# Two layers of graph attention on one core: PSUM banks swapped by batch parity, the order of pieces changed around projection, v and gather

## The chip, the cores and the metric

One core of a Trainium2 chip. The metric is the device time of the whole program in microseconds (us), as the median of several runs. The engines are named as in the profile: PE (TensorE), PEld (its weight loads), DVE (VectorE), ACT (ScalarE), POOL (GpSimd), SPq (the queue that issues DMAs).

## The reference, cut to what matters

Two residual layers with layer norm over 32 batches of 512 nodes and 512 features. The first is a graph layer (`l0` below), the second 8-head attention with a mask.

```python
# layer 0
mi = einsum('bkd,od->bko', x, Wi); mj = einsum('bkd,od->bko', x, Wj)
deg = a.sum(axis=1)
x = layernorm(x + deg[None, :, None] * (mi + b) + einsum('ij,bjo->bio', a, mj))
# layer 1: q, k, v = h @ W*.T + b*, 8 heads of 64
scores = where(adj == 0, -inf, q k^T / 8); attn = softmax(scores)
x = layernorm(x + (attn v) @ Wo.T + bo)
```

## The kernel before

Each 512x512x512 product (l0, q, k, v, output projection "pj") is done with seven half-size products, the **pieces** 1, 2, 6, 7, 4, 5, 3, in that order. Pieces {1, 2}, {6, 7, 4} and {5, 3} each add up in one PSUM bank; after each piece the bank is read by ACT or DVE before the next piece may write there. Two banks, "a" and "b", are all that pieces and gathers have. Weights of a piece come through a ring of 12 tiles in SBUF; its DMAs are issued by SPq in order, each waiting until the piece that used the tile is done.

Attention of batch b runs in 8 steps (two per head pair). Each step has scores, `exp` (ACT), mask (DVE) and attention times v ("ov" tiles); between them, PE does the pieces of batches n and n - 2 of the other layer parts. The list of pieces is cut into these 8 steps by the pieces' summed cost, so a piece that is moved can fall into another step.

Names used below: k6 is piece 6 of the product k; p1 is the copy of piece 1 that later pieces add; POOL's "differences" are the operands of the pieces; HT and OT are h and the attention output, turned (transposed); `base` is DVE's x + deg b, the start of the l0 output. "By starts" means that a pause is the time from one row's start to the next, less the undisturbed time. A "restart" is the 0.10 us that the piece behind a pause takes longer. "Half clock" is a stretch in which the trace records a granted TensorE clock of 0.5; nearly all are 3.41 us long or a multiple of it.

The parts that the argument touches, with cuts marked `# ...`:

```python
def load_x(b):
    XT[b] = work([P, NC, D], "xh", 3)
    nc.sync.dma_start(XT[b], rows(x[b]))

def l0_gather(b, dc, adjT=None):          # x^T, and A x in two fp32r halves
    pt = turn_tile()
    for jc in range(NC):
        nc.tensor.transpose(pt[...], xt[:, jc, dc * P:(dc + 1) * P], ident)     # L292
    nc.vector.tensor_mul(XD[b][:, dc, :], pt, deg_r)
    pm = mm_tile("b")
    # ... 4 matmuls with the rounded half xhi, 4 with the rest xlo (L299)
    nc.scalar.copy(AX_T[b][:, dc, :], pm)

def phase_a(n):     # gather of batch n among the last five k pieces of batch n - 1
    # ...
    for i in range(max(len(g), len(k))):
        res += k[i:i + 1] + g[i:i + 1]                                          # k in bank a, g in b

def phase_c(n):
    # ...
    res = [norm[0], norm[1], z(apply, n, 1)] if n else []
    res += [pc("v", n, 1, "a"), pc("q", n, 1, "b")]
    # ...
    for i in ORDER[2:]:                                                         # 6, 7, 4, 5, 3
        for f in pc("q", n, i, "b"), pc("v", n, i, "a"):
            res += [f] + [g for g in side[:1] if g]
            side = side[1:]
        if i == 5 and n + 1 < B:
            res += [z(load_x, n + 1)] if n > 0 else []                          # the load of the next batch
    if n + 1 < B:
        res += [z(ahead, n + 1)]                                                # casts of its first two blocks
    return res
```

Of the kernel before, what the change touches and what calls it, by code (L numbers as in the profile page):

```python
# [25 lines left out]
def gnn_attention_kernel(  # L26
# [57 lines left out]
    def mm_tile(bank):  # L84
        return psum.tile([P, 512], FT, name="mm" + bank, bufs=1)
# [194 lines left out]
        for ic in range(2 * half, 2 * half + 2):  # L280
            ln_apply(MV.pop((b, ic)), XT[b][:, ic, :])

    def l0_gather(b, dc, adjT=None):


        xt = XT[b]
        if dc == 0:
            XD[b] = big()
            AX_T[b] = big()
        pt = turn_tile()  # L290
        for jc in range(NC):
            nc.tensor.transpose(pt[:, jc * P:(jc + 1) * P], xt[:, jc, dc * P:(dc + 1) * P], ident)  # L292
        nc.vector.tensor_mul(XD[b][:, dc, :], pt, deg_r)  # L293
        pm = mm_tile("b")
        if adjT is None:
            parts = SPLIT.pop((b, dc))
            for w in range(2):
                for jc in range(NC):
                    nc.tensor.matmul(pm, parts[w][:, jc, :], adjR[:, jc, :],  # L299
                                     start=(w == 0 and jc == 0), stop=(w == 1 and jc == NC - 1))  # L300
        else:
            for jc in range(NC):
                nc.tensor.matmul(pm, xt[:, jc, dc * P:(dc + 1) * P], adjT[:, jc, :],
                                 start=(jc == 0), stop=(jc == NC - 1))
        nc.scalar.copy(AX_T[b][:, dc, :], pm)
        if adjT is None and dc + 2 < DC:
            split(b, dc + 2)
# [126 lines left out]
    def presum(hp, half):  # L434

        if half == 0:
            ES[hp] = work([P, 2, N], "es", 1)
            nc.gpsimd.tensor_add(ES[hp], E[0], E[1])  # L438
        else:
            for kc in (2, 3):  # L440
                nc.vector.tensor_add(ES[hp], ES[hp], E[kc])  # L441

    def values(b, hp, half):
        if half == 0:
# [27 lines left out]
        nc.vector.tensor_mul(OT[b, hp // 2][:, hp % 2, :], PV[hp], RL[hp][1])  # L472

    def rest(b, hp):
        return [(invert, b, hp, c) for c in range(4)] + [(tell, b, hp), (scale, b, hp)]

    def store(b):
        nc.sync.dma_start(rows(out[b]), XT.pop(b))
# [6 lines left out]
    def z(f, *a):  # L485
        return (0.0, f, *a)
# [4 lines left out]
    ORDER = (1, 2, 6, 7, 4, 5, 3)  # L491
    ALONE = ((1, "a"), (6, "b"), (2, "a"), (7, "b"), (5, "a"), (4, "b"), (3, "a"))

    def phase_a(n):

        g = [(TR + GA, l0_gather, n, dc) for dc in range(DC)] if n < B else []
        k = [pc("k", n - 1, i, "a") for i in ORDER[2:]] if n > 0 else []
        res = []
        for i in range(max(len(g), len(k))):
            res += k[i:i + 1] + g[i:i + 1]  # L500
            if n == 1 and i in (1, 3):
                res += [z(combine, "wo", nc.vector, i // 2)]
            if i == 1 and g:
                res += [z(combos, TX, n, lambda j, m: quarter(XD[n], j, m), (1,)),
                        z(combos, TA, n, lambda j, m: quarter(AX_T[n], j, m), (1,))]
        if g:
            res += [z(combos, TX, n, lambda j, m: quarter(XD[n], j, m), (2,)),
                    z(combos, TA, n, lambda j, m: quarter(AX_T[n], j, m), (2,)),
                    z(base, n, 0),
                    z(combos, TX, n, lambda j, m: quarter(XD[n], j, m), (3, 4)),  # L510
                    z(combos, TA, n, lambda j, m: quarter(AX_T[n], j, m), (3, 4)),
                    z(base, n, 1)]
        if n == 1:
            res += [z(fold)]
        return res

    def first():


        g = [(TR + GA, l0_gather, 0, dc) for dc in range(DC)]  # L520
        half = lambda name, i: z(combine, name, nc.gpsimd if name in ("wi", "wj") else nc.vector, i)
        y = [(8 * PC / 4, plain, ic) for ic in range(NC)]
        n = [(TR, l0_norm, 0, ic) for ic in range(NC)]
        return [g[0], z(graph_forms, 3), g[1], g[2], half("wv", 0), g[3], z(base, 0, 0), z(base, 0, 1), half("wv", 1),
                y[0], half("wq", 0), half("wi", 0), y[1], half("wq", 1), half("wi", 1), y[2], half("wk", 0), half("wj", 0),
                n[0], y[3], half("wk", 1), half("wj", 1), n[1]]

    def plain(ic):

        pm = mm_tile("ab"[ic % 2])  # L530
        c = slice(ic * P, (ic + 1) * P)
        for j, (t, w) in enumerate(((XD[0], W["wi"]), (AX_T[0], W["wj"]))):
            for dc in range(DC):
                nc.tensor.matmul(pm, t[:, dc, c], w[dc // 2][:, dc % 2, :], start=(j + dc == 0), stop=(j == 1 and dc == DC - 1))
        y = XT[0][:, ic, :]
        nc.vector.tensor_add(y, y, pm)
        mv = work([P, 5], "mv", 12)
        ln_stats(mv, y)
        ln_apply(mv, y)

    def project(m, i):

        res = [pc("pj", m, i, "b")]
        if i == 1:
            res = [z(combos, TO, m, ot_quarter(m), (1,))] + res
        if i == 2:
            res = [FLUSH] + res + [z(combos, TO, m, ot_quarter(m), (2, 3, 4))]
        return res

    def phase_b(n):  # L550

        m = n - 2
        if m < 0:
            res = []
            side = [z(add_bo, 0, i) for i in range(2)]
            for i, bank in (ALONE[0:1] + ALONE[2:3] + ALONE[1:2] + ALONE[3:]):
                res.append(pc("l0", n, i, bank))
                if i == 4:
                    res += [z(stats, n, 0)]
                res += side[:1]  # L560
                side = side[1:]
            return res + [z(apply, n, 0), z(stats, n, 1)]
        res = []
        for i in ORDER:
            res.append(pc("l0", n, i, "a"))
            if i == 4:
                res.append(z(stats, n, 0))
            if i == 5:
                res.append(z(stats, m, 0))
            if i == 3:  # L570
                res.append(z(stats, n, 1))
            res += project(m, i)
            if i == 4:
                res.append(z(apply, n, 0))
            if i in (7, 4):
                res.append(z(add_bo, n - 1, int(i == 4)))
        return res

    def phase_c(n):

        m = n - 2
        norm = [(TR, l0_norm, n, ic) for ic in range(NC)]
        h = lambda j, i: quarter(HT[n], j, i)
        res = [norm[0], norm[1], z(apply, n, 1)] if n else []
        res += [pc("v", n, 1, "a"), pc("q", n, 1, "b")]
        if m >= 0:
            res += [z(stats, m, 1)]
        res += [pc("v", n, 2, "a"), norm[2], norm[3], z(combos, TH, n, h, (1, 2)), pc("k", n, 1, "a"),
                z(combos, TH, n, h, (3, 4)), pc("q", n, 2, "b"), pc("k", n, 2, "a")]
        side = []  # L590
        if n == 0:

            side = [z(graph_forms, 2), None, z(graph_forms, 0), None, z(graph_forms, 1)]
        if m >= 0:
            res += [z(apply, m, 0), z(apply, m, 1), z(store, m)]
        for i in ORDER[2:]:
            for f in pc("q", n, i, "b"), pc("v", n, i, "a"):
                res += [f] + [g for g in side[:1] if g]
                side = side[1:]
            if i == 5 and n + 1 < B:  # L600
                res += [z(load_x, n + 1)] if n > 0 else []
        if n + 1 < B:
            res += [z(ahead, n + 1)]
        return res

    def fold():

        pd = mm_tile("b")
        bv_w = work([P, DC, P], "big", 6)
        for dc in range(DC):  # L610
            nc.vector.tensor_scalar(bv_w[:, dc, :], ones, bv_c[:, dc:dc + 1], None, op0=OP.mult)
            nc.tensor.matmul(pd, bv_w[:, dc, :], W["wo"][dc // 2][:, dc % 2, :], start=(dc == 0), stop=(dc == DC - 1))
        nc.vector.tensor_add(bo_r, bo_r, pd)

    def by_steps(todo):
        total, done, at, res = sum(f[0] for f in todo), 0.0, 0, []
# [68 lines left out]
    for n in range(1, B + 1):  # L685
        b = n - 1
        extra = []
        for step in range(STEPS):
# [9 lines left out]
            elif b > 0:  # L698
                values(b - 1, HP - 1, 1)
                sums(b - 1, HP - 1)  # L700
                extra = rest(b - 1, HP - 1)
            late = [(presum, hp, half)]
            for f in PERIODS[n][step]:
                if f is FLUSH:
                    some = len(extra)
                else:
                    run(f)

                    some = 0 if f[0] == 0.0 else len(extra) if step == 0 else max(1, round(f[0] / PC))
                if some:  # L710
                    for g in late + extra[:some]:
                        g[0](*g[1:])
                    late, extra = [], extra[some:]
            for g in late + extra:
                g[0](*g[1:])
            extra = []
# [15 lines left out]
    with tc.If(flag > 0), tc.tile_pool(name="general", bufs=1) as pools.work:  # L732
# [26 lines left out]
        with tc.For_i(0, B, 1) as b:  # L759
# [1 line left out]
            xt = XT[g] = work([P, NC, D], "xh", 1)  # L761
            nc.sync.dma_start(xt, x[bass.ds(b, 1)].rearrange("o (c p) d -> p (o c) d", p=P))
            for dc in range(DC):
                l0_gather(g, dc, adj_t)
            base(g, 0)
            base(g, 1)
            for ic in range(NC):
# [98 lines left out]
```

## Time and profile before

| | before |
|---|---|
| median of runs | 3995.48 us (3993.76 to 3996.59, 4 runs) |
| PE, DVE, POOL, ACT busy | 97, 65, 46, 27% |
| one steady batch, load to load | 122.41 us (mean of 29) |
| PE waiting for x in it | 0 |
| half-clock windows in the steady part | none |

PE is the bound. How it is read, and which pauses PE has, stands in the prediction with its lines. PE's recurring waits, from the list of waits before (total us of idle, times, longest), in the order k6, v2, q5, v1 and projection 2:

```profile
PE mma L375 <- DVE v L403: 24.2, 31, 0.8
PE mma L375 <- ACT p L382: 20.6, 30, 0.7
PE mmb L375 <- DVE q L418: 15.3, 30, 0.5
PE mma L375 <- ACT big L321: 10.9, 30, 4.0
...
PE mmb L375 <- DVE oT L472: 4.7, 30, 0.2
```

One caution for reading on: a row of the timeline gives a busy length that overlaps the next row (a piece is shown as 1.89 us but takes 1.73 from start to start), so pauses below are worked out from starts, and the bracket at the end of a row (idle before it) comes out some 0.17 us smaller.

### The profile page before, as it was taken

What the parts mean: (1) busy time and instruction counts of PE and PEld (TensorE: products, weight loads), DVE (VectorE), ACT (ScalarE), POOL (GpSimd) and SP (SyncE); (2) the same over time, 40 slices, a digit from 0 to 9 for tenths busy, and PEclk for the clock granted to TensorE, in tenths of its full rate; (3) what the DMA queues carried; (4) which work ended last, traced back from release to release, by engine and by line L of the source; (5) the groups of instructions that cost most, each with busy time, mean ns of one, the idle gap of its engine ahead of it and who ended that gap; (6) DMA issues with size and microseconds to landing.
All of it is one profiled execution on the core that took longest, in us unless ns stands there. A gap on an engine that the chain in (4) does not pass through costs nothing.

```text
span 3992.5 us, 46921 instructions
## 1 busy us (share of the span) xinstructions
PE 3869.0 (97%) x17370; PEld 2641.8 (66%) x17370; DVE 2611.4 (65%) x3525; ACT 1058.9 (27%) x1476; POOL 1846.2 (46%) x1861
## 2 busy tenths in 40 slices
PE   8999999999999999999999999999999999999997
PEld 6666666666666666666666666666666666666663
DVE  4566666666666666666666666666666666666666
ACT  2222222222322222222223222222222222222222
POOL 3354434544444544345444455443454434554433
PEclk9999999999999999999999999999999999999998
DMA  7323333333333333332333433333323333333330
GB/s 248 94 91 116 106 111 119 93 108 111 106 116 106 98 111 111 108 119 87 114 109 103 124 100 103 107 111 111 117 89 116 104 108 122 100 101 111 107 107 22
DMA packets 281865, 433.87 MB, mean 109 GB/s; under 512 B 23072, under 2 KB 119840, under 8 KB 281632
## 3 DMA queue, kind: packets, MB, share of 16 engines
q1 hardware_dynamic: 281376, 430.27, 35.0%
q8 instruction: 142, 2.33, 0.2%
q14 instruction: 91, 0.75, 0.1%
q0 software_dynamic: 256, 0.53, 0.0%
HBM read 389.29 MB, written 41.42 MB: 108 GB/s over the span
## 4 chain that ended last, share of the span: by engine, by line
PE 75%; DVE 18%; POOL 3%; issue 2%; ACT 2%; DMA 0%; SPq 0%; POOLq 0%
PE mma L375 31%; PE mmb L375 14%; PE sc L427 10%; PE ov L449 9%; PE mmb L299 6%; DVE xh L312 5%; DVE e L432 4%; DVE rl L462 3%; PE ov L456 2%; DVE es L441 2%; PE sc L292 1%; POOL mv L268 1%; DVE st L265 1%; POOL mv L267 1%; PE sc L320 1%
## 5 line engine op out<-in xcount | busy, mean ns | idle before, releaser
L375 PE MATMUL mma<-ring,big 128*128 128x256 f32 x5224 | 1216.3, 382 | 31.7 <-ACT p L382 20.6
L375 PEld LDWEIGHTS mma<-ring,big 128*128 128x128 f32 x5224 | 979.6, 190 | 255.9 <-DVE e L432 49.5
L431 ACT ACTIVATE sc<-sc 128x1024 f32<-128x1024 f32 x512 | 492.7, 1006 | 1546.0 <-PE sc L427 1467.6
L432 DVE TENSOR_TENSOR e<-sc,edge 128x1024 f32<-128x1024 f32 x512 | 602.7, 1218 | 368.7 <-ACT sc L431 368.7
L438 POOL TENSOR_TENSOR es<-e 128x1024 f32<-128x1024 f32 x128 | 301.6, 2356 | 896.4 <-PE ov L456 894.5
L344 POOL TENSOR_TENSOR big<-big 128x512 f32<-128x512 f32 x376 | 511.6, 1385 | 217.8 <-DVE big L293 195.8
L427 PE MATMUL sc<-q,k 64*128 64x512 f32 x2048 | 508.9, 615 | 0.2 <-ACT big L321 0.2
L449 PE MATMUL ov<-e,v 128*64 128x512 f32 x2048 | 497.6, 607 | 6.5 <-DVE told L467 6.5
L462 DVE RECIPROCAL rl<-ov 128x128 f32<-128x128 f32 x512 | 455.0, 924 | 5.4 <-PE ov L456 1.6
L375 PE MATMUL mma<-big,ring 128*128 128x256 f32 x1792 | 430.2, 383 | 27.9 <-DVE v L403 24.2
L375 PE MATMUL mmb<-big,ring 128*128 128x256 f32 x1792 | 427.8, 382 | 15.3 <-DVE q L418 15.3
L375 PEld LDWEIGHTS mma<-big,ring 128*128 128x128 f32 x1792 | 331.9, 190 | 111.5 <-DVE v L403 36.7
L375 PEld LDWEIGHTS mmb<-big,ring 128*128 128x128 f32 x1792 | 339.0, 190 | 73.3 <-DVE q L418 27.3
L267 POOL TENSOR_SCALAR mv<-mv 128x1 f32<-128x1 f32 x256 | 80.8, 316 | 618.0 <-DVE mv L266 604.4
L449 PEld LDWEIGHTS ov<-e,v 128*64 128x64 f32 x2048 | 124.6, 136 | 347.6 <-issue 294.8
L441 DVE TENSOR_TENSOR es<-es,e 128x1024 f32<-128x1024 f32 x256 | 326.8, 1277 | 4.4
L427 PEld LDWEIGHTS sc<-q,k 64*128 64x128 f32 x2048 | 176.1, 186 | 209.3 <-issue 195.8
L390 POOL TENSOR_TENSOR xh<-xh,p 128x512 f32<-128x512 f32 x186 | 230.6, 1268 | 117.4 <-ACT p L382 117.4
L393 DVE TENSOR_TENSOR xh<-xh,mma 128x512 f32<-128x512 f32 x186 | 125.7, 676 | 225.5 <-PE mma L375 220.0
L184 POOL TENSOR_TENSOR xlo<-xh,xhi 128x512 fp32r<-128x512 f32 x128 | 162.7, 1281 | 238.7 <-ACT xhi L183 238.7
L272 ACT ACTIVATE xh<-xh,mv 128x512 f32<-128x512 f32 x256 | 198.4, 811 | 240.2 <-POOL mv L269 224.6
L375 PE MATMUL mmb<-ring,big 128*128 128x256 f32 x1032 | 251.6, 387 | 4.9 <-POOL big L344 4.9
(125 smaller groups left out, 3696.3 us busy)
## 6 DMA issues: line engine op xcount, KB each, us to landing
ring<-wq SPq DMA_DIRECT2D x160, 256.0 KB, 2.6
ring<-wv SPq DMA_DIRECT2D x160, 256.0 KB, 2.6
ring<-wk SPq DMA_DIRECT2D x160, 256.0 KB, 4.1
ring<-wi SPq DMA_DIRECT2D x155, 256.0 KB, 2.6
ring<-wj SPq DMA_DIRECT2D x155, 256.0 KB, 2.8
ring<-wo SPq DMA_DIRECT2D x155, 256.0 KB, 2.6
xh<-in_x_dram SPq DMA_DIRECT2D x32, 1024.0 KB, 5.5
out_dram<-xh SPq DMA_DIRECT2D x31, 1024.0 KB, 5.1
```

The costliest lines, as they stand in the source:

```text
L299: nc.tensor.matmul(pm, parts[w][:, jc, :], adjR[:, jc, :], start=(w == 0 and jc == 0), stop=(w == 1 and jc == NC - 1))
L312: nc.vector.scalar_tensor_tensor(y, b0_r, deg_c[:, ic:ic + 1], y, op0=OP.mult, op1=OP.add)
L344: nc.gpsimd.tensor_tensor(dst, p, q, op=OP.subtract)
L375: nc.tensor.matmul(pm[:, c * Q:(c + 1) * Q], lhs, rhs, start=first, stop=(kc == 1 and n == len(terms) - 1), skip_group_check=True)
L390: nc.gpsimd.tensor_tensor(d, d, p1, op=OP.add)
L427: nc.tensor.matmul(ps[:, s, :], KT[b, hp // 2][r, hp % 2, kc * P:(kc + 1) * P], QT[b, hp // 2][r, hp % 2, :], start=True, stop=True)
L431: nc.scalar.activation(ps, ps, AF.Exp, scale=QSCALE)
L432: nc.vector.tensor_tensor(e, ps, edge[:, kc:kc + 1, :].to_broadcast([P, 2, N]), op=OP.mult)
L438: nc.gpsimd.tensor_add(ES[hp], E[0], E[1])
L441: nc.vector.tensor_add(ES[hp], ES[hp], E[kc])
L449: nc.tensor.matmul(PV[hp][s * HD:(s + 1) * HD, :], V[b][:, kc, c0:c0 + HD], E[kc][:, s, :], start=(kc == 0), stop=(kc == NC - 1))
L462: nc.vector.reciprocal(rl[:, c], pl[:, c])
```

## The change

Its intent is to take away PE's small recurring pauses: banks swap roles with each batch's parity, so that between the last v piece and the first k piece (k6), which share a bank, the gather of the next batch runs in the other one; the first two blocks of h are turned during the output projection, not right ahead of v; the first l0 piece moves ahead of the last k; v's bias is folded into the output bias early; DVE's two sums of a head pair are emitted one at a time; and the scaling of the attention output goes ahead of its check ("tell"). Cut to the core:

```diff
+    def banks(n):
+        return ("a", "b") if n % 2 == 0 else ("b", "a")
 # phase_a: g in bank A, k in bank K
-            res += k[i:i + 1] + g[i:i + 1]
+            res += g[i:i + 1] + k[i:i + 1]
 # ...
+        return res + [ ... z(base, n, 1), pc("l0", n, 1, A), k[4]]
 # phase_b
+            if i == 3:
+                res += [z(stats, n, 1), (TR, l0_norm, n, 1)]
+            if i == 5:
+                res.append((TR, l0_norm, n, 0))
 # phase_c
-        res = [norm[0], norm[1], z(apply, n, 1)] if n else []
-        res += [pc("v", n, 1, "a"), pc("q", n, 1, "b")]
+        res = [pc("v", n, 1, A)] + ([z(apply, n, 1)] if n else []) + [pc("q", n, 1, K)]
 # rest
-        ... + [(tell, b, hp), (scale, b, hp)]
+        ... + [(scale, b, hp), (tell, b, hp)]
 # steps
-            late = [(presum, hp, half)]
+            late = [(presum, hp, 0)] if half == 0 else [(presum, hp, 2), (presum, hp, 3)]
 # first(): fold of v's bias ahead of the first v, in place of the end of phase_a(1)
```

More of the change, by code (lines that the diff above doesn't have):

```diff
@@ L281, in apply, with l0_gather @@
             ln_apply(MV.pop((b, ic)), XT[b][:, ic, :])
-    def l0_gather(b, dc, adjT=None):
+    def l0_gather(b, dc, bank, adjT=None):
         xt = XT[b]
@@ L293, in l0_gather @@
         nc.vector.tensor_mul(XD[b][:, dc, :], pt, deg_r)
-        pm = mm_tile("b")
+        pm = mm_tile(bank)
         if adjT is None:
@@ L439, in presum @@
         else:
-            for kc in (2, 3):
-                nc.vector.tensor_add(ES[hp], ES[hp], E[kc])
+            nc.vector.tensor_add(ES[hp], ES[hp], E[half])
     def values(b, hp, half):
@@ L474, in rest @@
     def rest(b, hp):
-        return [(invert, b, hp, c) for c in range(4)] + [(tell, b, hp), (scale, b, hp)]
+        return [(invert, b, hp, c) for c in range(4)] + [(scale, b, hp), (tell, b, hp)]
     def store(b):
@@ L492, in gnn_attention_kernel @@
     ALONE = ((1, "a"), (6, "b"), (2, "a"), (7, "b"), (5, "a"), (4, "b"), (3, "a"))
+    def banks(n):
+        return ("a", "b") if n % 2 == 0 else ("b", "a")
     def phase_a(n):
-        g = [(TR + GA, l0_gather, n, dc) for dc in range(DC)] if n < B else []
-        k = [pc("k", n - 1, i, "a") for i in ORDER[2:]] if n > 0 else []
+        A, K = banks(n)
+        if n == B:
+            return [pc("k", n - 1, i, bank) for i, bank in ((6, K), (7, K), (5, A), (4, K), (3, A))]
+        xq, aq = lambda j, m: quarter(XD[n], j, m), lambda j, m: quarter(AX_T[n], j, m)
+        g = [(TR + GA, l0_gather, n, dc, A) for dc in range(DC)]
+        k = [pc("k", n - 1, i, K) for i in ORDER[2:]]
         res = []
-        for i in range(max(len(g), len(k))):
-            res += k[i:i + 1] + g[i:i + 1]
+        for i in range(DC):
+            res += g[i:i + 1] + k[i:i + 1]
             if n == 1 and i in (1, 3):
                 res += [z(combine, "wo", nc.vector, i // 2)]
-            if i == 1 and g:
-                res += [z(combos, TX, n, lambda j, m: quarter(XD[n], j, m), (1,)),
-                        z(combos, TA, n, lambda j, m: quarter(AX_T[n], j, m), (1,))]
-        if g:
-            res += [z(combos, TX, n, lambda j, m: quarter(XD[n], j, m), (2,)),
-                    z(combos, TA, n, lambda j, m: quarter(AX_T[n], j, m), (2,)),
-                    z(base, n, 0),
-                    z(combos, TX, n, lambda j, m: quarter(XD[n], j, m), (3, 4)),
-                    z(combos, TA, n, lambda j, m: quarter(AX_T[n], j, m), (3, 4)),
-                    z(base, n, 1)]
-        if n == 1:
-            res += [z(fold)]
-        return res
+            if i == 1:
+                res += [z(combos, TX, n, xq, (1,)), z(combos, TA, n, aq, (1,))]
+        return res + [z(combos, TX, n, xq, (2,)), z(combos, TA, n, aq, (2,)), z(base, n, 0),
+                      z(combos, TX, n, xq, (3, 4)), z(combos, TA, n, aq, (3, 4)), z(base, n, 1),
+                      pc("l0", n, 1, A), k[4]]
     def first():
-        g = [(TR + GA, l0_gather, 0, dc) for dc in range(DC)]
+        g = [(TR + GA, l0_gather, 0, dc, "b") for dc in range(DC)]
         half = lambda name, i: z(combine, name, nc.gpsimd if name in ("wi", "wj") else nc.vector, i)
@@ L524, in first @@
         return [g[0], z(graph_forms, 3), g[1], g[2], half("wv", 0), g[3], z(base, 0, 0), z(base, 0, 1), half("wv", 1),
-                y[0], half("wq", 0), half("wi", 0), y[1], half("wq", 1), half("wi", 1), y[2], half("wk", 0), half("wj", 0),
-                n[0], y[3], half("wk", 1), half("wj", 1), n[1]]
+                y[0], z(scaled, 0), half("wq", 0), half("wi", 0), y[1], z(scaled, 1), half("wq", 1), half("wi", 1), z(fold, 0), y[2], half("wk", 0), half("wj", 0),
+                z(scaled, 2), n[0], y[3], half("wk", 1), half("wj", 1), n[1], (2 * PC, fold, 1), z(scaled, 3)]
     def plain(ic):
@@ L536, in plain, with scaled @@
         nc.vector.tensor_add(y, y, pm)
-        mv = work([P, 5], "mv", 12)
-        ln_stats(mv, y)
-        ln_apply(mv, y)
+        MV[0, ic] = work([P, 5], "mv", 12)
+        ln_stats(MV[0, ic], y)
+    def scaled(ic):
+        ln_apply(MV.pop((0, ic)), XT[0][:, ic, :])
     def project(m, i):
-        res = [pc("pj", m, i, "b")]
+        res = [pc("pj", m, i, banks(m)[1])]
         if i == 1:
@@ L555, in phase_b @@
             side = [z(add_bo, 0, i) for i in range(2)]
-            for i, bank in (ALONE[0:1] + ALONE[2:3] + ALONE[1:2] + ALONE[3:]):
+            A, K = banks(n)
+            for i, bank in ((2, A), (6, K), (5, A), (7, K), (3, A), (4, K)):
                 res.append(pc("l0", n, i, bank))
@@ L561, in phase_b @@
                 side = side[1:]
-            return res + [z(apply, n, 0), z(stats, n, 1)]
-        res = []
-        for i in ORDER:
-            res.append(pc("l0", n, i, "a"))
+            return res + [z(apply, n, 0), z(stats, n, 1), (TR, l0_norm, n, 0), (TR, l0_norm, n, 1)]
+        res = project(m, 1)
+        for i in ORDER[1:]:
+            res.append(pc("l0", n, i, banks(n)[0]))
             if i == 4:
@@ L570, in phase_b @@
             if i == 3:
-                res.append(z(stats, n, 1))
+                res += [z(stats, n, 1), (TR, l0_norm, n, 1)]
             res += project(m, i)
@@ L583, in phase_c @@
         h = lambda j, i: quarter(HT[n], j, i)
-        res = [norm[0], norm[1], z(apply, n, 1)] if n else []
-        res += [pc("v", n, 1, "a"), pc("q", n, 1, "b")]
+        A, K = banks(n)
+        res = [pc("v", n, 1, A)] + ([z(apply, n, 1)] if n else []) + [pc("q", n, 1, K)]
         if m >= 0:
             res += [z(stats, m, 1)]
-        res += [pc("v", n, 2, "a"), norm[2], norm[3], z(combos, TH, n, h, (1, 2)), pc("k", n, 1, "a"),
-                z(combos, TH, n, h, (3, 4)), pc("q", n, 2, "b"), pc("k", n, 2, "a")]
+        res += [pc("v", n, 2, A), norm[2], norm[3], z(combos, TH, n, h, (1, 2)), pc("k", n, 1, A),
+                z(combos, TH, n, h, (3, 4)), pc("q", n, 2, K), pc("k", n, 2, A)]
         side = []
@@ L596, in phase_c @@
         for i in ORDER[2:]:
-            for f in pc("q", n, i, "b"), pc("v", n, i, "a"):
+            for f in pc("q", n, i, K), pc("v", n, i, A):
                 res += [f] + [g for g in side[:1] if g]
@@ L604, in phase_c, with fold @@
         return res
-    def fold():
-        pd = mm_tile("b")
-        bv_w = work([P, DC, P], "big", 6)
-        for dc in range(DC):
-            nc.vector.tensor_scalar(bv_w[:, dc, :], ones, bv_c[:, dc:dc + 1], None, op0=OP.mult)
-            nc.tensor.matmul(pd, bv_w[:, dc, :], W["wo"][dc // 2][:, dc % 2, :], start=(dc == 0), stop=(dc == DC - 1))
-        nc.vector.tensor_add(bo_r, bo_r, pd)
+    def fold(part):
+        if part == 0:
+            bv_w = OPEN["fold"] = work([P, DC, P], "rl", 1)
+            for dc in range(DC):
+                nc.vector.tensor_scalar(bv_w[:, dc, :], ones, bv_c[:, dc:dc + 1], None, op0=OP.mult)
+        else:
+            pd = ov_tile()
+            for dc in range(DC):
+                nc.tensor.matmul(pd, OPEN["fold"][:, dc, :], W["wo"][dc // 2][:, dc % 2, :], start=(dc == 0), stop=(dc == DC - 1))
+            nc.vector.tensor_add(bo_r, bo_r, pd)
     def by_steps(todo):
@@ L710, in gnn_attention_kernel @@
                 if some:
-                    for g in late + extra[:some]:
+                    for g in late[:1] + extra[:some]:
                         g[0](*g[1:])
-                    late, extra = [], extra[some:]
+                    late, extra = late[1:], extra[some:]
             for g in late + extra:
@@ L763, in gnn_attention_kernel @@
             for dc in range(DC):
-                l0_gather(g, dc, adj_t)
+                l0_gather(g, dc, "b", adj_t)
             base(g, 0)
```

## The prediction

> **What bounds the kernel now.** I read the page first (shares, then the chain), then the timeline of TensorE (PE) in one steady batch, then the DVE, ACT and issue-queue (SPq) timelines at the places where PE paused.
>
> ```profile
> PE 3869.0 (97%) x17370; PEld 2641.8 (66%) x17370; DVE 2611.4 (65%) x3525; ACT 1058.9 (27%) x1476; POOL 1846.2 (46%) x1861
> ...
> PE 75%; DVE 18%; POOL 3%; issue 2%; ACT 2%; DMA 0%; SPq 0%; POOLq 0%
> ```
>
> PE is the bound. No other engine is above 65%, and no DMA is on the chain, so the time is PE's issue rate plus its pauses. From one x load to the next the trace repeats every 122.35 us. The change removes no matmuls in a batch; only pauses can change. The PE timeline round the x load (start, length; each x8 row is one "piece" of four fp32 matmuls):
>
> ```profile
> 1293.22 1.89 PE L375 MATMUL mma<-ring,big 128*128 128x256 f32 x8
> 1295.62 1.99 PE L375 MATMUL mmb<-big,ring 128*128 128x256 f32 x8 [0.51 <-DVE q L418]
> 1297.45 1.89 PE L375 MATMUL mma<-ring,big 128*128 128x256 f32 x8
> 1299.17 1.89 PE L375 MATMUL mmb<-big,ring 128*128 128x256 f32 x8
> 1300.99 1.99 PE L427 MATMUL sc<-q,k 64*128 64x512 f32 x8
> ...
> 1305.64 1.99 PE L375 MATMUL mma<-ring,big 128*128 128x256 f32 x8
> 1308.41 1.99 PE L375 MATMUL mma<-big,ring 128*128 128x256 f32 x8 [0.78 <-DVE v L403]
> 1310.24 0.60 PE L292 MATMUL sc<-ident,xh 128*128 128x128 f32 x4
> ```
>
> These rows are v4, q5, v5, q3, scores, v3, k6 and the transposes of the next batch's x. An undisturbed piece takes 1.73 us start to start (1297.45 to 1299.17). After v3 it is 2.77: k6 takes v3's bank and waits for its last read. Every pause also makes the next piece 1.83 instead of 1.73. Measured start to start over the free pace, a steady batch has five pauses: k6 0.94, v2 0.85 (waits for p1's copy), q5 0.67, v1 0.40 (waits for HT's copy), output projection 2 0.32 (waits for OT). That is 3.18, with five restarts of 0.10 some 3.7 us per batch. The changes of array shape around scores and values remain.
>
> **The skill.** "TensorE: Matmul & The Clock Gate", in "Step-by-step: what each phase is for", says that matmuls stay in program order and only weight loads are pulled ahead: one that waits for data holds all behind it. The trace agrees: k6's 0.94 delays everything after it. The same page, "What's actually happening", says that PE's clock is halved after an idle window of about 3.4 us. Here the 3.95 us pause at 54 us is followed by a piece of 2.94 us start to start (59.54 to 62.48) instead of 1.73, and the recorded half-clock stretches are 3.413 us or multiples. Cutting the span into such windows, those with PE busy 34% or less were followed by half clock, those with 49% or more were not. "DMA: Bandwidth & Descriptors", "Rules for kernel authors": issue a load early, wait late. The kernel before does so by little, see below.
>
> **The change part by part (per steady batch, 30 of them).**
>
> *Removed.* Banks by parity: after v3 comes the gather of the next batch (2.28 us: 0.35 transposes, 1.02 and 0.91 matmuls) in the other bank, so k6 finds v3's bank read: -0.94 -0.10. First two blocks of h turned during the projection: v1 no longer follows the HT copy directly, -0.40 -0.10, and the apply pair (2 x 0.81 on ACT) is put behind p1's copy, so v2 doesn't wait: -0.85 -0.10. q5 now stands one step later behind scores and values (3.8 us) and v4, and DVE's two sums of 1.24 are apart: -0.67 -0.10. Sum -3.26.
>
> *OT.* Scaling ahead of the tell saves 0.61 on DVE (the tell starts at 1220.78, the product behind it at 1221.39). But the first l0 piece (3.45 us) moved from between the sums and projection 2 to the end of the batch before. From the scores' start: base (6.27 us on DVE) now starts before that l0 piece and ends at about 3.4; k3's reads 0.9, masks 2.3, four reciprocals 3.4, product 0.65: 10.6. PE wants it at 10.15 (1.92 + 1.77 + 0.96 + 1.83 + 3.45 + 0.2). Pause 0.5 to 0.6 instead of 0.32: **+0.25**.
>
> *q1.* Step 3 now opens with a transpose, and one sum goes behind it and ahead of the read of projection 3. In DVE's row at this place:
>
> ```profile
> 1258.84 2.36 DVE L432 TENSOR_TENSOR e<-sc,edge 128x1024 f32<-128x1024 f32 x2 [0.17 <-ACT sc L431]
> 1261.11 0.68 DVE L265 BATCH_NORM_STATS2 st<-xh 128x6 f32<-128x512 f32 x1
> ...
> 1262.72 0.65 DVE L393 TENSOR_TENSOR xh<-xh,mmb 128x512 f32<-128x512 f32 x1
> 1263.30 2.48 DVE L441 TENSOR_TENSOR es<-es,e 128x1024 f32<-128x1024 f32 x2
> ```
>
> the read (L393) stands before both sums; after, it stands behind one. Masks end 4.75 us after the scores' start, statistics 6.3, sum 7.55, read 8.1. q1 takes the bank that the projection left, and PE is there at 7.8 (1.92 + 1.87 + 0.44 + 1.83 + 1.73). **+0.4 +0.1.**
>
> *The x load.* This is what I believe decides. The load is issued after v5 in both kernels, in order with the weight prefetches, the last of which waits for v5's matmuls:
>
> ```profile
> 1299.37 0.37 SPq L253 DMA_DIRECT2D ring<-in_wjT_dram  x1
> 1299.85 0.41 SPq L107 DMA_DIRECT2D xh<-in_x_dram  x1
> ```
>
> ACT's cast of it, and the page's row of this load (KB each, median us to landing):
>
> ```profile
> 1305.28 1.14 ACT L183 CAST xhi<-xh 128x512 fp32r<-128x512 f32 x2 [1.18 <-DMA xh<-in_x_dram]
> ...
> xh<-in_x_dram SPq DMA_DIRECT2D x32, 1024.0 KB, 5.5
> ```
>
> Issue is 0.68 after q3's start; it lands 5.2 to 7.3 us later in the steady part, mean about 5.65. Before, PE reaches the transposes 10.4 us after the issue, because scores, values, sums (4.65), v3 and k6 lie between: nobody waits. After, the built order on PE is v4, q5, v5, q3, v3, gather: PE is there 3.45 us after q3's start, 2.77 after the issue. Pause 5.65 + 0.1 - 2.77 = 2.95. Then the transposes (0.35) run while ACT casts the first half (0.62): +0.3; and POOL's subtraction (1.27) ends 0.3 after the first four gather matmuls: +0.3. Restart 0.1. **+3.65.** Such a gap leaves many a 3.4 us window under about 40% busy: a gap of 2.95 with 0.3 behind it does so in about 80% of the positions of the window, and a half-clock window costs up to 1.7, partly inside the gap, say 1.3. **+1.0.**
>
> Rest (norm 1 against the first mask, projection 6 against POOL's difference): +0.1.
>
> Sum per batch: -3.26 + 0.25 + 0.5 + 3.65 + 1.0 + 0.1 = +2.2; times 30 = **+67 us**.
>
> *Start and end.* Before, v's bias is folded alone behind base:
>
> ```profile
> 115.10 6.12 PE L612 MATMUL mmb<-xh,big 128*128 128x512 f32 x8 [7.75 <-DVE big L611]
> ```
>
> 7.9 us of pause, and 6.12 instead of 3.43 at half clock. Folded ahead of the first v, it also fills the 3.95 us pause that the first v has at 54 us (4.1 start to start, 1.7 of half clock behind it). At most -16; at the end two of the last k's waits (1.15 each) go with alternating banks: -2. I take **-18**.
>
> 3996.6 + 67 - 18 = 4045.6; I put 4044.
>
> **The rivals.** (1) *The pauses go and nothing comes.* Then 3996.6 - 18 - 30 x 3.3 = 3880, -2.9%. For it: the intended effects are sound. Against it: it needs the load to land within 2.8 us of the issue; the fastest of the steady part took 5.2. (2) *The load waits, but the clock holds and q1 and OT pass.* Then -3.26 + 3.65 + 0.1 = +0.5 per batch: 3994. Steady pauses before were never over 1 us, so the steady part tells nothing of the clock; only start and end do. (3) *DVE becomes the bound.* Its order changes in steps 0, 3 and 7, and each queue slips by up to one op (1.2 us) more than I worked out: +2 per batch more, 4105. For it: the two DVE chains above are longer than PE's time. Against it: DVE is busy 65% and stands idle in between. (4) *The weight ring*: same number of transfers of 2.6 us, same depth of 12; nothing changes there.
>
> **Range and chances.** The load's wait is nearly certain in kind; its size is 3.1 to 4.2. The clock adds 0 to 1.7, DVE's two places 0.2 to 1.6. Per batch +0.5 to +3.2 about, 80% range 4005 to 4080. Over 2% slower begins at 4076.5: 0.16. Over 2% faster would need rival 1: 0.04.
>
> **What would show it.** The first transposes (L292) of a batch idle about 3 us before them, ended by the x load, 30 times, about 90 us in all; the wait for k6 on v's last read, and those of v2 and v1, gone from the list of waits; ACT's cast then within 0.1 us of the transposes; half-clock windows (tenths under 9 or a mean granted clock near 0.98) in the steady part; a wait of q1 on the projection's read of 0.4; bias fold without 7.75 us. The prediction is wrong if the load lands earlier than the transposes, if PE has no gap there, or if the period of a batch comes out under 122.35.

## The result, and the profile after

4048.32 us (4046.68 to 4050.38, 4 runs) against 3995.48: ratio 1.0133, 95% interval 1.0115 to 1.015. Ratios here are the mean time of one kernel's runs over that of the other's of the same rounds, so not quite the ratio of the medians. The change is slower, by 53 us: clear of the noise, though under 2%.

The page of the profile after, busy times and the chain that ended last, by engine and by line:

```profile
PE 3902.1 (96%) x17370; PEld 2663.9 (66%) x17370; DVE 2595.3 (64%) x3525; ACT 1058.3 (26%) x1476; POOL 1862.8 (46%) x1861
...
PE 72%; DVE 11%; POOL 9%; DMA 4%; issue 2%; ACT 1%; SPq 0%; POOLq 0%
PE mma L375 20%; PE mmb L375 20%; PE sc L427 10%; PE ov L448 9%; POOL xh L390 5%; DMA xh<-in_x_dram 4%; PE mmb L299 3%; PE mma L299 3%; DVE rl L461 3%; PE ov L455 2%; DVE st L265 2%; DVE xh L393 2%; POOL big L344 2%; DVE e L432 2%; POOL es L438 2%
```

As many matmuls as before, but a DMA has come onto the chain with 4% of the span: the load of x. Its place in PE's timeline of one batch (start, length):

```profile
1180.76 1.89 PE L375 MATMUL mmb<-ring,big 128*128 128x256 f32 x8
1182.48 1.89 PE L375 MATMUL mma<-big,ring 128*128 128x256 f32 x8
1184.21 1.89 PE L375 MATMUL mmb<-ring,big 128*128 128x256 f32 x8
1188.77 1.11 PE L292 MATMUL sc<-ident,xh 128*128 128x128 f32 x4 [2.67 <-DMA xh<-in_x_dram]
1189.53 2.06 PE L299 MATMUL mma<-adjR,xhi 128*128 128x512 f32 x4
1191.39 1.24 PE L299 MATMUL mma<-adjR,xlo 128*128 128x512 f32 x4
```

The issue queue and ACT at the same place:

```profile
1182.68 0.37 SPq L253 DMA_DIRECT2D ring<-in_wjT_dram  x1
1183.14 0.42 SPq L107 DMA_DIRECT2D xh<-in_x_dram  x1
```

```profile
1188.75 1.14 ACT L183 CAST xhi<-xh 128x512 fp32r<-128x512 f32 x2 [12.23 <-DMA xh<-in_x_dram]
```

These are v5, q3, v3 and then the gather. The load is issued as before, 0.66 us after q3's start. PE is done with v3 at 1185.94 (1184.21 + 1.73), the load lands at 1188.72, and the transposes start at 1188.77: 2.83 us of pause. The first matmuls of the gather then take 1.86 us where they took 1.01 before (1310.60 to 1311.61 there): a half-clock window stands behind the gap.

The recurring waits for p1, for q5's bank, for k6's bank and for HT that stood in the list before are gone. PE's recurring waits in the list of the kernel after are these. None of them recurs in the list before (POOL's L344 stands there once, at the end, with 4.9); OT's wait goes on, but is too short for this list:

```profile
PE sc L292 <- DMA xh<-in_x_dram: 89.3, 30, 5.5
...
PE mmb L375 <- POOL big L344: 7.9, 15, 5.0
...
PE mma L375 <- POOL big L344: 2.9, 14, 0.2
PE mmb L375 <- DVE xh L393: 2.4, 15, 0.2
PE mma L375 <- DVE xh L393: 2.2, 14, 0.2
```

By the trace's starts, the x wait is 3.13 us per batch (2.45 to 5.65). 21 of the 29 steady batches have a half-clock stretch at the gap (3.41 us, or 6.83 in three). Where a batch has none, its length less its own x wait is the same every time, which separates the wait from the clock (load to load, us):

| length | x wait | difference |
|---|---|---|
| 123.37 | 2.61 | 120.76 |
| 123.85 | 3.08 | 120.77 |
| 123.33 | 2.61 | 120.72 |
| 123.47 | 2.73 | 120.74 |
| 123.77 | 3.01 | 120.76 |
| 123.32 | 2.56 | 120.76 |

So a batch costs 120.74 (the mean of all eight such batches) + the x wait. The mean of all is 124.62 = 120.74 + 3.13 + 0.75, and 0.75 is the half clock: 1.04 us for each of the 21 batches that have it.

### The profile page after: what moved, and what is told of

Same layout as the page of the kernel before. It is cut to its first block, busy times and chain, and to the rows that moved or that the text cites. A ratio compares the mean times of both kernels' runs of the same rounds, so it can differ in the third digit from the quotient of the medians.

```text
span 4048.5 us, 46895 instructions
## 1 busy us (share of the span) xinstructions
PE 3902.1 (96%) x17370; PEld 2663.9 (66%) x17370; DVE 2595.3 (64%) x3525; ACT 1058.3 (26%) x1476; POOL 1862.8 (46%) x1861
## 4 chain that ended last, share of the span: by engine, by line
PE 72%; DVE 11%; POOL 9%; DMA 4%; issue 2%; ACT 1%; SPq 0%; POOLq 0%
PE mma L375 20%; PE mmb L375 20%; PE sc L427 10%; PE ov L448 9%; POOL xh L390 5%; DMA xh<-in_x_dram 4%; PE mmb L299 3%; PE mma L299 3%; DVE rl L461 3%; PE ov L455 2%; DVE st L265 2%; DVE xh L393 2%; POOL big L344 2%; DVE e L432 2%; POOL es L438 2%
## 5 line engine op out<-in xcount | busy, mean ns | idle before, releaser
L375 PE MATMUL mmb<-ring,big 128*128 128x256 f32 x3144 | 734.6, 382 | 7.9 <-POOL big L344 7.9
L375 PE MATMUL mma<-ring,big 128*128 128x256 f32 x3112 | 724.2, 381 | 3.1 <-POOL big L344 2.9
L375 PEld LDWEIGHTS mmb<-ring,big 128*128 128x128 f32 x3144 | 593.2, 191 | 131.4 <-DVE e L432 23.5
L375 PEld LDWEIGHTS mma<-ring,big 128*128 128x128 f32 x3112 | 584.7, 190 | 125.4 <-DVE e L432 25.2
L344 POOL TENSOR_TENSOR big<-big 128x512 f32<-128x512 f32 x376 | 549.7, 1488 | 222.3 <-DVE big L293 177.9
L267 POOL TENSOR_SCALAR mv<-mv 128x1 f32<-128x1 f32 x256 | 50.3, 196 | 747.2 <-DVE mv L266 737.1
L440 DVE TENSOR_TENSOR es<-es,e 128x1024 f32<-128x1024 f32 x256 | 339.6, 1327 | 0.1
L393 DVE TENSOR_TENSOR xh<-xh,mmb 128x512 f32<-128x512 f32 x186 | 125.7, 676 | 217.4 <-PE mmb L375 216.4
```

The source lines that it names most:

```text
L344: nc.gpsimd.tensor_tensor(dst, p, q, op=OP.subtract)
L375: nc.tensor.matmul(pm[:, c * Q:(c + 1) * Q], lhs, rhs, start=first, stop=(kc == 1 and n == len(terms) - 1), skip_group_check=True)
L393: nc.vector.tensor_tensor(d, d, pm, op=OP.add)
L440: nc.vector.tensor_add(ES[hp], ES[hp], E[half])
```

## The experiments

**Theory**: the load of x, still issued after v5, no longer has scores, values, sums and k6 between its issue and the first use (q3 and v3 alone are left), and this wait with the half clock behind it is the whole loss. **Rival**: the rearranged DVE and POOL chains cost it, and the load would be made up elsewhere. The first four runs tell these apart; the next ones undo parts of the change where the load doesn't cover them.

**The load after v4 in the changed kernel.**

```diff
-            if i == 5 and n + 1 < B:
+            if i == 4 and n + 1 < B:
```

> The changed kernel with the x load issued one round of q and v earlier (after v4 in place of v5), nothing else. PE then reaches the transposes of the next batch 2.77 + 3.45 = 6.2 us after the issue. Theory (the load's wait and the half clock it brings are the loss): the wait of 3.13 us falls to about 0.2 (only the loads slower than 6.2 us), the half-clock windows (0.76 per batch) and the cast's waits (about 0.45) go: 4048 - 30 x 4.1 = 3925 us (3908 to 3935), below the kernel before. Rival (the rearranged DVE and POOL chains of steps 0 and 3 are the loss, the load would have been made up elsewhere): 4048, within 15 us.

Measured: correct, 3915.96 us (3914.27 to 3916.89), ratio to before 0.9802 (0.9786 to 0.9819); granted clock 0.996 in place of 0.986. In its list of waits the row is

```profile
PE sc L292 <- DMA xh<-in_x_dram: 0.9, 1, 0.9
```

Once in place of 30 times. One changed number gives back 132 us, so theory stands and the rival falls. The mean steady batch is 120.36 us: the 120.74 from above less 0.4, part of the waits for the casts of x. The rest of them goes where the load lands earlier still (120.11 in the next run). The wait and the half clock went together here; no run takes away one alone, so their shares come from the table above.

**The load after v7.** The same with `i == 7`.

> The changed kernel with the load issued three rounds earlier by program order, after v7. The store of the batch before last lands some 9.3 us ahead of the issue in the changed kernel, so the load can go about 9 us earlier at most and the issue queue waits about 2 us for that store. Theory: no wait for x is left at all, 4048 - 30 x (3.13 + 0.76 + 0.45) = 3918 (3905 to 3930), 0 to 8 us below the version with the load after v4. Rival (earlier loads hold up the weight prefetches in the same queue): weights late, over 3935.

Measured: 3913.14 us (3912.26 to 3914.45), ratio 0.9796 (0.978 to 0.9813); the mean steady batch is 120.11 us. No wait for x at all, and no late weights in PE's list of waits. Both versions with an earlier load beat the kernel before by 2.0%. This kernel is the ground for the runs below.

**The load late in the kernel before.** Nothing of the change; `i == 3` in the kernel before.

> The kernel before with its load issued later (after v3 in place of v5), nothing of the change in it. PE then reaches the transposes about 2.1 us after the issue in place of 10.4. Theory: a wait of about 5.75 + 0.1 - 2.1 = 3.7 us appears, with 0.5 for casts and restart and 0.9 of half clock: 3996 + 30 x 5.1 = 4150 (4115 to 4170). Rival (a late load is hidden or made up): 3996, within 20.

Measured: 4139.92 us (4134.72 to 4140.71), ratio 1.036 (1.0343 to 1.0377), granted clock 0.987. Its list of waits now has the same row as that of the kernel after:

```profile
PE sc L292 <- DMA xh<-in_x_dram: 94.3, 29, 4.5
```

A mean pause of 3.37 us where 3.7 was expected, and half clock in 15 of 29 batches: the late load alone, in a kernel that has none of the new order, makes this loss and more.

**k ahead of the gather.** The gather is turned back behind k6, banks still by parity.

```diff
-            res += g[i:i + 1] + k[i:i + 1]
+            res += k[i:i + 1] + g[i:i + 1]
```

> The changed kernel with the order of gather and k pieces turned back (k6 ahead of the first gather), banks by parity kept. k6 then follows v3 in the same bank and waits 0.94 + 0.10 again, but PE reaches the transposes 2.77 us later: the wait for x falls from 3.13 to about 0.4 and is too short for a half-clock window. Theory: per batch -2.7 - 0.75 + 1.05 = -2.4, 3976 us (3960 to 3990). If the half clock is not tied to the length of the gap, 0.75 x 30 = 22 more, 3998.

Measured: 3993.61 us (3993.26 to 3995.83), ratio 0.9999. The edit did more than was meant: the border between two steps lies one item behind v3, so the first gather went over it, behind k6 and behind the next step's scores, values and sums. PE now reaches the transposes 10.3 us after the issue, and the load lands 3.4 us or more ahead of them in all of the 30 batches but the first:

```profile
PE sc L292 <- DMA xh<-in_x_dram: 0.8, 1, 0.8
```

```profile
1418.03 1.99 PE L375 MATMUL mmb<-big,ring 128*128 128x256 f32 x8 [0.78 <-DVE v L403]
1419.95 1.99 PE L427 MATMUL sc<-q,k 64*128 64x512 f32 x8
...
1424.60 0.66 PE L292 MATMUL sc<-ident,xh 128*128 128x128 f32 x4
```

There isn't one half-clock window in the steady part. But a gap of 0.4 us had been expected and none was left, so the run says nothing on how short a gap is harmless. It is one more kernel in which the load has its slack back and both the wait and the half clock are gone. The time is still 18 us over what was expected. The PE timeline shows why:

```profile
1321.03 3.72 PE L375 MATMUL mmb<-ring,big 128*128 128x256 f32 x16 [0.67 <-ACT big L305]
...
1343.08 1.99 PE L375 MATMUL mma<-ring,big 128*128 128x256 f32 x8 [1.40 <-POOL big L344]
```

The fourth gather is now right ahead of the first l0 piece, in the same bank, which therefore waits for the copy of the gather (0.85 by starts); and POOL, whose chain hangs on that copy, is later for the projection's sixth piece (1.57 where the kernel after has 0.37). I had counted only the waits at the place that I moved, and had missed that the gather falls into the next step. This run would have been misread as "the rival is right" from its time alone.

**h turned at v again** (from here on, each run undoes one part on top of the kernel with the load after v7, 3913 us).

```diff
-        res = [pc("v", n, 1, A)] + ([z(apply, n, 1)] if n else []) + [pc("q", n, 1, K)]
+        res = ([norm[0], norm[1], z(apply, n, 1)] if n else []) + [pc("v", n, 1, A), pc("q", n, 1, K)]
```

and the two turns in phase b taken out.

> From here on each run undoes one part of the change on top of the changed kernel with the load after v7 (3913 us, 120.1 us per batch). Here the first two blocks of h are turned right ahead of the first v again, with the apply pair between, as before the change. If the part was worth what the trace of before showed (v1 0.40, v2 0.85, restarts 0.2) and the 0.32 + 0.1 of q1 goes with it because the sum stands behind the projection's read again: +1.03 x 30 = +31, 3944 (3935 to 3958). Rival (the waits would be hidden now anyway): 3913.

Measured: 3946.92 us (3944.75 to 3947.51), so +34. The size is as expected, but not the wait:

```profile
1357.24 1.94 PE L448 MATMUL ov<-e,v 128*64 128x512 f32 x8
1360.01 0.66 PE L320 MATMUL sc<-ident,xh 128*128 128x128 f32 x4 [0.83 <-DVE e L432]
1361.14 0.66 PE L320 MATMUL sc<-ident,xh 128*128 128x128 f32 x4 [0.47 <-DVE e L432]
```

With the other pieces in their new places the two turns come right behind values, and wait 0.90 and 0.64 by starts for the masks that free their PSUM tile, not for h's copy or p1. So turning h early is worth what was said in this order too, but this run doesn't confirm the mechanism of before; the lists of waits before and after, shown above, do: the two waits are in the one and not in the other.

**Banks fixed.** `banks` returns ("a", "b") for every batch.

> The swap of banks by parity undone: every batch uses the same bank for l0, v and gather, the other for projection, q and k; the new order of pieces stays. The gather's matmuls then follow v3 in v3's bank. v's last read takes 0.94, the transposes ahead of the gather cover 0.35 of it: +0.6 + 0.1 per batch, +20, 3933 (3926 to 3940). Rival (the order alone is enough, the gather's position hides it): 3913.

Measured: 3932.35 us (3930.8 to 3932.98), +19. The line that was expected is there, 0.67 by starts over the free pace:

```profile
1394.07 0.60 PE L292 MATMUL sc<-ident,xh 128*128 128x128 f32 x4
1395.10 1.17 PE L299 MATMUL mma<-adjR,xhi 128*128 128x512 f32 x4 [0.43 <-DVE v L403]
```

So of the 0.94 that k6 lost before, the new order alone would have taken somewhat under a third (the transposes), and the parity the other 0.67.

**Sums together.** `late` emits both sums at the first piece of a step again.

> DVE's two sums of a head pair emitted together again. In step 3 both (2.5 us) then stand ahead of the projection's read and q1 waits 1.24 longer; in step 5 both stand ahead of q5's read and q3, which adds to the same bank, waits about 0.75 + 0.1. +2.1 x 30 = +63, 3976 (3950 to 3985). Rival (DVE makes it up, only q1): 3950. Sums apart worth nothing: 3913.

Measured: 3970.63 us (3967.95 to 3974.78), +57: the two places that were named, 1.58 and 1.62 by starts, in the PE timeline of one batch (the first is 1.58 in every batch; the second is 1.62 in 13 of 29 and 0.67 in 15):

```profile
1368.85 1.99 PE L375 MATMUL mma<-big,ring 128*128 128x256 f32 x8 [1.42 <-DVE xh L393]
...
1402.78 1.99 PE L375 MATMUL mma<-big,ring 128*128 128x256 f32 x8 [1.46 <-DVE q L418]
```

Per batch this is 1.26 more for q1 and 1.1 on average for q5, less OT's wait and restart (0.40), which go; the batch is 1.88 longer (121.99 against 120.11). Of the parts that were undone singly this is worth most. The new places of the projection and l0 pieces were undone in no run.

**Tell first.** `rest` with the tell ahead of the scaling again.

> The tell ahead of the scaling again. Projection 2 waits 0.61 longer for OT, the wait goes from 0.29 to 0.9, restart the same: +0.61 x 30 = +18, 3931 (3926 to 3938). Rival (OT's wait is set by another engine): 3913.

Measured: 3915.43 us (3913.98 to 3917.35), +2, where +18 was expected. The wait for OT did grow by 0.61, to 0.91 by starts, as worked out:

```profile
1308.21 0.59 PE L375 MATMUL mma<-ring,oT 128*128 128x256 f32 x2
1309.55 1.56 PE L375 MATMUL mma<-ring,oT 128*128 128x256 f32 x6 [0.74 <-DVE oT L471]
1310.95 3.62 PE L375 MATMUL mmb<-ring,big 128*128 128x256 f32 x16
1314.40 1.89 PE L375 MATMUL mma<-ring,big 128*128 128x256 f32 x8
```

But the projection's sixth piece (last row) starts 3.45 after the one ahead of it, without its pause of 0.37 and the restart of 0.10: PE comes later, and POOL's difference is ready. Of two waits in a row on chains that don't get shorter, the second shrinks as the first grows; they don't add up. My expectation counted one of them alone.

**Two of the new waits mended, with the load after v7**.

```diff
+            done = 0
             for f in PERIODS[n][step]:
 # ...
+                if half == 1 and f[1] is l0_norm:
+                    some = 0                       # a turn calls for no sum
                 if some:
-                    for g in late[:1] + extra[:some]:
+                    done += f is not FLUSH
+                    hold = step == 0 and n >= 3 and done < 4    # POOL's sum behind the differences
+                    for g in late[:1 - hold] + extra[:some]:
                         g[0](*g[1:])
-                    late, extra = late[1:], extra[some:]
+                    late, extra = late[1 - hold:], extra[some:]
```

> The changed kernel with the load after v7 and two waits mended: in step 3 the transpose no longer calls for a sum, so that projection 3 is read before both sums (q1 waited 0.32 + 0.10), and POOL's sum of step 0 goes behind the differences that projection 6 waits for (0.37 + 0.10). Theory: -0.89 x 30 = -27, 3886 (3880 to 3900), ratio to before 0.973. Rival (one wait hides the next, as the tell did: PE comes earlier to a chain that doesn't get shorter): only q1's goes, 3900, or less.

Measured: correct, 3889.88 us (3888.96 to 3891.85), ratio to before 0.9736 (0.972 to 0.9753). Both waits are gone; the mean steady batch is 119.18 us, 0.93 less, and the only recurring pause of PE that is left beside the changes of array shape is OT's 0.30. This is the fastest of all runs: 2.6% under before, 3.9% under the change as it was made (3889.88 over 4048.32). They were run at other times.

**The control: an earlier load in the kernel before.** `i == 7` there.

> The kernel before with its load issued after v7, nothing else: the control to the two versions of the changed kernel with an earlier load. Theory: no wait for x was there, so nothing is gained: 3995, within 5. Rival (an earlier load helps by itself, e.g. its casts on ACT and POOL come earlier): 3980 or below.

Measured: 3996.07 us (3992.95 to 3999.58), ratio 1.0002. An earlier load has no value by itself; it had one only after the change.

**The fold at the end again,** on the kernel with the load after v7: `fold` out of `first()`, back behind the last k of the first period.

> On the changed kernel with the load after v7: the fold of v's bias back at the end of the first period (behind base, the first l0 piece and the last k), the rest as changed. PE then waits for the fold's operands, which stand on DVE behind base (6.3 us) and k's reads: about 5 us of pause and 1.7 of half clock; and the first v, without the fold ahead of it, waits about 1 us for the copy of h. +7.5, 3921 (3916 to 3927). Rival (the place of the fold is free since other pieces now fill the gap): 3913.

Measured: 3920.97 us (3920.03 to 3922.37), +8, with the wait of the old place back at 5.34 by starts, with half clock behind it:

```profile
112.04 5.73 PE L619 MATMUL ov<-xh,rl 128*128 128x512 f32 x8 [5.18 <-DVE rl L615]
```

## Why the prediction was right, point by point

The time (4044 predicted, 4048.32 measured) and the per-batch sum (+2.2 predicted; 124.62 - 122.41 = 2.21 measured) agree. How far each term carries that:

- **The x wait.** +2.95 was put for the pause, 3.13 measured. The term was a little small because the loads took 5.88 us to land on average, not 5.65; one took 8.40. (Its sum is off by a little, too: 5.65 + 0.1 - 2.77 is 2.98.) For the casts behind it 0.6 was put; in the undisturbed-clock batch at 1312.76 us the first transposes to the first matmul take 0.65 (0.36 without a wait) and the four matmuls behind 1.37 (1.02), together 0.64; the kernel with the load after v7, which has neither, is 0.63 below the 120.74. Shown by the trace, by the run with the load after v4, and the other way round by the late load in the kernel before.
- **The half clock.** +1.0 was put (80% of batches at 1.3); 0.75 measured (21 of 29 at 1.04). The kind was right, the size a third too large. The rule behind it (windows with PE busy 34% or less are followed by half clock, those with 49% or more not) comes out of the trace before, within a point, for windows at full clock (but for the one at the start, ahead of PE's first work). It leaves out windows already at half clock: the one from 3943.0 us, with PE busy 78%, was followed by half clock again.
- **The five pauses that go.** k6, v1, v2 and q5 are gone from the waits. The change without the x wait is 120.11 us per batch against 122.41: 2.30 less. It pays 0.42 for q1 and 0.47 for projection 6, and OT gained 0.03, so the removed pauses come to about 3.16 (2.30 + 0.42 + 0.47 - 0.03), where the prediction had 3.26.
- **OT.** Here a step failed: "Pause 0.5 to 0.6 instead of 0.32". Measured 0.29. The chain of base, k3's reads, masks, reciprocals and product was right: in the batch shown below the product ends 10.59 us after the scores' start, 10.6 was worked out. Wrong was when PE wants it. Projection 2 starts at 9.93, and its first two matmuls (0.43) do not need this product, as the x2 of its row before shows too; the third, which does, is free at 10.36, not 10.15, and starts at 10.65:

```profile
1096.07 1.99 PE L427 MATMUL sc<-q,k 64*128 64x512 f32 x8
...
1105.97 0.69 DVE L471 TENSOR_TENSOR oT<-ov,rl 128x512 f32<-128x512 f32 x1
1106.00 2.28 PE L375 MATMUL mma<-ring,oT 128*128 128x256 f32 x8
```

- **q1.** +0.4 put, 0.32 measured, on the wait that was named (projection 3 read behind one sum). In DVE's timeline the sum of 1148.32 stands ahead of the read, and PE follows the read:

```profile
1148.32 1.19 DVE L440 TENSOR_TENSOR es<-es,e 128x1024 f32<-128x1024 f32 x1
1149.43 0.68 DVE L393 TENSOR_TENSOR xh<-xh,mma 128x512 f32<-128x512 f32 x1
1150.03 1.24 DVE L440 TENSOR_TENSOR es<-es,e 128x1024 f32<-128x1024 f32 x1
```

```profile
1148.12 1.89 PE L375 MATMUL mmb<-ring,big 128*128 128x256 f32 x8
1150.17 1.99 PE L375 MATMUL mma<-big,ring 128*128 128x256 f32 x8 [0.16 <-DVE xh L393]
```

- **The rest**, "+0.1", was mis-sized: projection 6 waits 0.37 and a restart for POOL's difference. It balances OT. The agreement of the sum is partly luck of that kind.
- **Start and end.** -18 was put. Up to the issue of the second batch's load the kernel after is 12.2 us ahead (184.90 against 197.09). The fold's pause (7.9) and the half clock at it, and the pause at the first v, are gone as said, but the first batch brings a new one that I hadn't looked for, since there the early turn of h comes right behind the applying of its norm, with no piece between:

```profile
143.58 0.95 PE L320 MATMUL sc<-ident,xh 128*128 128x128 f32 x4 [2.86 <-ACT xh L272]
```

  From the last load to the end the kernel after takes 249.6 against 245.6. The thirtieth x wait (3.57), its casts (0.64) and its half clock (1.04) are in there, and three of the four last k waits are gone; a wait of 2.54 for OT at 3883.49 us with half clock behind it is new. The rest of the end was not traced. Less the thirtieth x wait with what hangs on it, start and end come to some -13, where -18 was put.

Check of the sum: 29 x 2.21 - 12.2 + 4.0 = 55.9, and the spans of the two profiled runs differ by 56.0 (4048.5 - 3992.5).

Of the rivals, the first ("the pauses go and nothing comes", 3880) is what the same change does with the load out of the way and its two new waits mended: 3890. It fell mainly because one line that the change didn't touch, the place of the load, had lost its slack of 4.7 us: with the load after v7 alone it is 3913. The second (the clock holds, q1 and OT pass) fell by the half clock and q1; OT did pass. The third (DVE the bound) was seen nowhere in the steady part except at q1. Of the fourth (the ring) there is no sign: no wait of PE for a DMA into the ring is in the list after.

## What to carry to other kernels

When pieces are moved, ask for each transfer that is *not* moved how much work still lies between its issue and its first use: here 10.4 us became 2.8 with no edit to the load. Read the pauses from start to start, and do not simply add two waits in a row: one that grew by 0.61 cost 2 us in all 30 batches here, because the next shrank. A gap of PE costs more than its length when it is long enough to halve the clock behind it: here 2.5 to 3 us often was.

## What the Trainium skill lacked or had wrong

- "TensorE: Matmul & The Clock Gate" puts the half clock after at least one idle window of about 3.4 us ("What's actually happening") and asks for no idle gaps over some 3 us ("Why this matters for your kernels"). Here the window need not be idle throughout, and shorter gaps did it. The steady part was cut into windows of 3.413 us in step with the half-clock stretches. Of the 20 windows at full clock that were followed by half clock, 17 had PE busy 8 to 41%, and three 43, 46 and 50%; three others with 42, 43 and 47% were not followed by it. Pauses of 2.45 and 2.62 us brought it, pauses of 2.61 and 3.08 did not: where the gap lies in the window decides. Cost: 1.04 us per batch that had it.
- No page gives a time for the second matmul of a piece behind a pause: it started 0.10 us late (0.32 in place of 0.216 from start to start) after each recurring wait of PE for a bank or an operand here, and as much when a piece followed split-array matmuls.
- "DMA: Bandwidth & Descriptors" ("Measured (HBM→SBUF, 128 partitions, SWDGE, issued from GpSimd)") gives 6.15 us for 1 MB as a span of the DMA engines. It is for another way of issuing. From the start of the issue on the SPq queue to the landing the 1 MB load took 5.2 to 8.4 us here, mean 5.88; no page gives that spread, and it decides how far ahead a load must be issued.
